# The slots layer of a decoder kernel issued in small parts between the half steps of the first cross attention

## The chip, the cores and the metric

The kernel runs on one core of one Trainium2 chip. The metric is the device time of one execution in microseconds (us). Five engines of the core work side by side, each through its own queue of instructions: PE (TensorE, matrix products and transposes), DVE (VectorE), ACT (ScalarE), POOL (GpSimd) and SP (SyncE, which here only starts transfers).

## The reference, cut to what matters

The input x has 64 batches of 128 rows and 256 columns, and all is fp32 but for two quantized products at the end. Six layers follow each other, each in the form x = x + layer(layernorm(x)):

```
x = x + window_attention(ln(x))          # stage A
x = x + cross_attention_0(ln(x), ctx)    # stage B: 16 heads of 16, mask, output projection
x = x + slots(ln(x))                     # stage C
x = x + causal_attention(ln(x))          # stage D: bias from a small net over positions
x = x + cross_attention_1(ln(x), ctx)    # stage E
x = x + bit_linear_ffn(ln(x))            # stage F
```

The slots layer (C) routes each row to 64 slots and writes back from them. For each batch:

```
h      = gelu(x @ w1' + c1)                       # 128 wide
logits = (h @ w2' + b2) / (|tau| + 0.1)           # 64 slots
alpha  = softmax over the top 8 logits, 0 elsewhere
gi     = (alpha^T @ x) / column sums of alpha     # 64 x 256
r, z   = sigmoid(...), n = tanh(...)              # a GRU step from gi and the fixed slot state
out    = alpha @ ((new slot state) @ wv' ) @ wo' + bo
```

No value of one batch enters another batch in any of the layers, so the slots layer of a batch needs only the cross attention of the same batch.

## The kernel before

**Groups and stages.** The 64 batches are held in SBUF as 16 tiles `x[g]` of four batches (`GB` = 4). The stages run one after the other, each over all groups, and each changes `x[g]` in place. Each has its own pools of SBUF and PSUM buffers. The program is written against a layer that records instructions, finds their dependences, sets the semaphores and gives out buffers; it also decides the order of the instructions on each engine, by priority (the order of the program's text) and by what its own plan holds to be ready. So an instruction may stand earlier on its engine than the text has it, but on the chip each engine works through that fixed order.

**Stage B, cross attention 0.** `stage_cross0` calls `attention_stage`, a software pipeline in half steps `j` = 0 to 136. A half step handles half of the heads (two of four row blocks) of a batch. In half step `j`:

- `score_burst` (L409) issues 32 small products into one PSUM tile `sc` of four banks: for batch `j // 2` the scores whose row maxima are needed, and for the batch three half steps older the transposed scores with the maxima already subtracted. Pool `scB` has one such tile, so a burst waits until the tile has been read.
- `score_max` (DVE, L424 `negmax`) reads two banks of it, `score_exp` (ACT, L438 `e`) the other two.
- Then come, for older batches, `weigh_values` (L459, at odd `j`), `divide` (L471 to L478), `turn_output` (L488) and `finish_batch` (L140, then the add into x at L619), each with a PSUM tile of the pool `ps`, which has four.
- At even `j`, `start` calls `prep` of the next batch: normalize the query (L594), copies on POOL (L599 to L604), eight transposes (L612) and two copies on ACT (L615). For the first batch of a group it also computes the group's layer norm statistics (`ln_stats`, L97 to L100, with a power on POOL), from which DVE takes `r4` (L588).
- At odd `j`, `shift_query` (L447, L451) waits for the maxima and makes the shifted query `q2`.

A batch is finished in half step 2n + 8. One group of four batches is eight half steps.

**Stage C, slots.** `stage_slots` runs over groups: `slots_route(g)`, then the two `slots_update` generators of group g - 1 (one for each pair of batches), which are advanced in turn. `slots_route` normalizes (L107), adds `bo` to x on POOL (L723), transposes (`transpose_group`, L119), projects and applies Gelu (L131, L731), makes the logits (L734 to L743), picks the top eight (L748, L749) and forms the softmax (L750 to L759, with an Exp at L754). `slots_update` has six parts between its `yield`s: u1 the sums into slots (L770), u2 their division (L776 to L779), u3 transposes, the copy `giT` and the products with `wih` (L783 to L798), u4 the gates on DVE, POOL and ACT (L802 to L810), u5 transposes, the copy `sT` and the product with `wvo` (L814 to L822), u6 the product with alpha and the add into x (L826, L831). Gelu and Exp belong to different activation tables, so ACT loads a table before each (L731 and L754).

**Stage D's start.** `prep_fire` builds a bias table: position differences on POOL (`Iota`, L895 and L899), absolute value, logarithm and relu on ACT (L904 to L911), a product on DVE (L910), 128 small products on PE (L918) and the adds on DVE (L926). Its tiles lie in SBUF that the stages before it used.

**Constants.** `prep_window`, `prep_cross0`, `prep_proj(.., "e")`, `prep_bitnet` and `prep_slots` load and prepare weights ahead of stage A. SP starts the transfers.

Of the kernel before, what the change touches and what calls it, by code (L numbers as in the profile page):

```python
# [16 lines left out]
D = 256  # L17
H = 16
DH = 16
S = 128  # L20
# [61 lines left out]
def psum(k):  # L82
    return k.ps.tile([128, 512], F, tag="ps", name="ps")
# [412 lines left out]
    b.fin(py[:, 0:D])  # L496


def attention_stage(k, pool, w1, prep, wo, lay, bias_s=None, bias_t=None):

    nms = []
    for i in range(2):
        t = w1.tile([S, lay.size], F, name=f"negmax{i}")
        k.nc.gpsimd.memset(t, 0.0)
        nms.append(t)
    bs = {}  # L510

    def start(n):
        b = bs[n] = prep(n)
        b.lay = lay
        b.nm = nms[n % 2]
        b.e = [None, None]

    def at(j, lag):
        n, odd = divmod(j - lag, 2)
        return bs.get(n) if not odd else None  # L520

    start(0)
    for j in range(2 * k.NB + 9):
# [12 lines left out]
        if at(j, 6):  # L536
            divide(k, pool, at(j, 6))
        if at(j, 7):
            turn_output(k, pool, at(j, 7))
        if at(j, 8):  # L540
            finish_batch(k, bs.pop((j - 8) // 2), wo)
        if hf == 0 and n + 1 < k.NB:
            start(n + 1)
        if hf == 1 and n < k.NB:
            shift_query(k, pool, bs[n])

# [9 lines left out]
    return cx  # L556


def stage_cross0(k, w):
    nc = k.nc  # L560
    with k.tc.tile_pool(name="wb", bufs=2) as wp, k.tc.tile_pool(name="wb1", bufs=1) as w1, \
            k.tc.tile_pool(name="wb3", bufs=3) as w3:
        qps, kps, vas = [], [], []
        for i in range(2):
            qp = w1.tile([S, H, 32], F, name=f"qp{i}")
            nc.gpsimd.memset(qp, 0.0)
            nc.gpsimd.memset(qp[:, :, 17:18], 1.0)
            qps.append(qp)
            kp = w1.tile([S, H, 32], F, name=f"kp{i}")
            nc.gpsimd.memset(kp, 0.0)  # L570
            nc.gpsimd.memset(kp[:, :, 16:17], 1.0)
            kps.append(kp)
        for i in range(4):
            va = w1.tile([S, H, 32], F, name=f"va{i}")
            nc.gpsimd.memset(va, 0.0)
            nc.gpsimd.memset(va[:, :, 16:17], 1.0)
            vas.append(va)
        cxs = {0: load_group(k, wp, 0)}
        stats = {}

        def prep(bi):
            g, b = divmod(bi, GB)
            if b == 0:
                if g + 1 < k.G:
                    cxs[g + 1] = load_group(k, wp, g + 1)
                mv, rs = ln_stats(k, wp, g)
                r4 = wp.tile([S, GB], F, tag="r4", name="r4")
                nc.vector.tensor_scalar(r4, rs, 0.25, None, ALU.mult)  # L588
# [12 lines left out]
            cv = cxs[g][:, b, :].rearrange("p (h d) -> p h d", d=DH)  # L601
            nc.gpsimd.tensor_copy(kp[:, :, 0:DH], cv)
            nc.gpsimd.tensor_copy(kp[:, :, 17], w.mbias[:, bi : bi + 1].to_broadcast([S, H]))
            nc.gpsimd.tensor_scalar(va[:, :, 0:DH], cv, mk, None, ALU.mult)  # L604
            t = Batch()
            t.qt = w3.tile([128, 4, S], F, tag="qt", name="qt")
            t.kt = w3.tile([128, 4, S], F, tag="kt", name="kt")
            for src, dst in ((qp, t.qt), (kp, t.kt)):
                p = psum(k)
                sf = src.rearrange("p h i -> p (h i)")  # L610
                for c in range(4):
                    nc.tensor.transpose(  # L612
                        p[:, c * S : (c + 1) * S], sf[:, c * 128 : (c + 1) * 128], k.ident
                    )
                nc.scalar.copy(dst, p.rearrange("p (c l) -> p c l", l=S))  # L615
            t.va, t.row_scale = va, mk

            def fin(y):
                nc.vector.scalar_tensor_tensor(xb, y, mk, xb, ALU.mult, ALU.add)  # L619

            t.fin = fin
            return t

        attention_stage(k, wp, w1, prep, w.wp, Heads(False))


def prep_cross0(k, pool):
# [87 lines left out]
    return w  # L715


def slots_route(k, w, g, wp):
    nc = k.nc
    xn = wp.tile([S, GB, D + 1], F, tag="xn", name="xn")  # L720
# [5 lines left out]
    xnT = wp.tile([128, 2, GB * S], F, tag="xnT", name="xnT")  # L726
    transpose_group(k, xn, xnT)
    p = psum(k)
    project(k, p, w.w1, 0, 128, xnT, 0, GB * S)
    hT = wp.tile([128, GB * S], F, tag="hT", name="hT")  # L730
    nc.scalar.activation(hT, p, AF.Gelu, bias=w.c1[:, 0:1])  # L731
    p = psum(k)
# [5 lines left out]
    lg = wp.tile([S, GB, SLOTS], F, tag="lg", name="lg")  # L738
# [4 lines left out]
    nc.vector.tensor_scalar(lg, lg, w.itau[:, 0:1], None, ALU.mult)  # L743
    m8 = wp.tile([S, GB, 8], F, tag="m8", name="m8")
    al = wp.tile([S, GB, SLOTS], F, tag="al", name="al")
    e = wp.tile([S, GB, SLOTS], F, tag="e", name="e")
    for b in range(GB):
        nc.vector.max(m8[:, b], lg[:, b])  # L748
        nc.vector.match_replace(al[:, b], m8[:, b], lg[:, b], -3.0e38)  # L749
    nc.vector.tensor_tensor(al, al, lg, ALU.not_equal)  # L750
    nc.vector.tensor_tensor(
        e, lg, m8[:, :, 0:1].to_broadcast([S, GB, SLOTS]), ALU.subtract
    )
    nc.scalar.activation(e, e, AF.Exp)  # L754
    nc.vector.tensor_tensor(al, al, e, ALU.mult)
    den = wp.tile([S, GB], F, tag="den", name="den")
    nc.vector.tensor_reduce(den, al, AX.X, ALU.add)
# [7 lines left out]
def slots_update(k, w, g, xn, al, pb, wp):  # L765
# [67 lines left out]

def stage_slots(k, w):
    with k.tc.tile_pool(name="wc", bufs=2) as wp, k.tc.tile_pool(name="wc4", bufs=4) as wq:
        prev = None
        for g in range(k.G + 1):
            cur = slots_route(k, w, g, wp) if g < k.G else None
            if prev is not None:
                parts = [slots_update(k, w, g - 1, *prev, pb, wq) for pb in range(GB // 2)]  # L840
                while parts:
                    parts = [q for q in parts if next(q, q) is not q]
            prev = cur

# [410 lines left out]
def decoder(tc, a, stages="ABCDEF"):  # L1255
# [152 lines left out]
```

## Time and profile before

| what | us |
|---|---|
| median of 3 runs (3829.28 to 3832.84) | 3831.49 |
| the profiled execution, its own time | 3831.31 |
| its span, first to last instruction | 3829.5 |
| stage B, from the first memsets of its buffers to the last add into x | 612 to 1183 |
| stage C, to the last add into x | 1183 to 1634 |
| preparation of stage D, to its first statistics | 1634 to 1697 |

A row of the timeline reads: start, duration, engine, line, operation, output <- input, and in brackets the idle time of the engine ahead of it with what ended it. A row of the waits reads: who waited for whom, us in total, how many times, the longest. A row of the windows reads: the stretch, its length, busy us of PE, PE's weight load, DVE, ACT and POOL with the number of instructions, the granted TensorE clock as a share of full speed, DMA share and GB/s. Durations of neighbours overlap by some 0.1 us, so two starts are the better measure of what an instruction takes of its engine.

### The profile page before, as it was taken

Reading aid. Unit: us, or ns where it says so; the run is one execution under the profiler, and the core shown is the slowest. Engines: PE = TensorE matmul, PEld = TensorE weight load, DVE = VectorE, ACT = ScalarE, POOL = GpSimd, SP = SyncE. Lnnn points to the kernel's source line nnn. Section 1 sums busy time; section 2 is a strip of 40 time slices with the busy share of each in tenths; the row PEclk is TensorE's granted clock in tenths of the full one; section 3 lists DMA queues with packets and bytes.
Section 4 is the critical chain, followed back from the end, with each engine's and each line's share of the span. In section 5 each row is a group of like instructions: output and inputs, shape, how many; then the busy total and the mean of one; then the engine's idle time right before and its main releaser. Section 6 shows DMA issues by size and latency. Waiting matters only on the chain.

```text
span 3829.5 us, 65173 instructions
## 1 busy us (share of the span) xinstructions
PE 2986.5 (78%) x27764; PEld 1889.1 (49%) x27764; DVE 2602.7 (68%) x4843; ACT 1279.2 (33%) x1882; POOL 1063.4 (28%) x1048
## 2 busy tenths in 40 slices
PE   4888885888887766658888888888888985776676
PEld 1333333666664333345666666666666762333333
DVE  5888766666666555447888777765556557887766
ACT  1111111444443232323333333334444543332332
POOL 3555553343332222130000000020001004534434
PEclk9898986999998888968999999899999997888887
DMA  5000000000000000000000000000000000000000
GB/s 182 1 1 1 1 1 17 18 18 13 18 13 1 1 1 1 1 15 1 1 2 1 1 2 1 2 28 13 13 13 18 13 2 6 11 11 17 11 17 17
DMA packets 40817, 48.09 MB, mean 13 GB/s; under 512 B 4448, under 2 KB 37616, under 8 KB 40272
## 3 DMA queue, kind: packets, MB, share of 16 engines
q1 hardware_dynamic: 39872, 42.17, 3.4%
q8 instruction: 220, 3.60, 0.4%
q0 software_dynamic: 656, 1.75, 0.2%
q14 instruction: 69, 0.57, 0.0%
HBM read 35.52 MB, written 8.39 MB: 11 GB/s over the span
## 4 chain that ended last, share of the span: by engine, by line
PE 29%; DVE 20%; ACT 3%; POOL 3%; issue 1%; DMA 0%; DVEq 0%; POOLq 0%; ACTq 0%; SPq 0%
PE sc L409 7%; PE ps L131 6%; PE cv L1142 4%; DVE uq L1194 3%; PE ps L140 3%; DVE negmax L424 3%; PE ps L990 3%; DVE sb L422 3%; DVE e L436 2%; POOL dg L1088 2%; PE ps L447 2%; PE ps L471 1%; PE ps L459 1%; DVE xn L107 1%; ACT e L438 1%
## 5 line engine op out<-in xcount | busy, mean ns | idle before, releaser
L409 PE MATMUL sc<-kt,qt 32*128 32x128 f32 x6144 | 508.6, 297 | 164.1 <-DVE e L436 104.7
L409 PEld LDWEIGHTS sc<-kt,qt 32*128 32x128 f32 x6144 | 421.0, 197 | 306.5 <-issue 177.3
L424 DVE TENSOR_REDUCE negmax<-sc 128x8 f32<-128x1024 f32 x256 | 313.3, 1224 | 298.7 <-PE sc L409 298.7
L409 PE MATMUL sc<-q,kt 32*128 32x128 f32 x6144 | 510.4, 298 | 1.9 <-DVE e L436 1.6
L409 PEld LDWEIGHTS sc<-q,kt 32*128 32x128 f32 x6144 | 421.0, 197 | 4.7 <-issue 2.9
L438 ACT ACTIVATE e<-sc 128x1024 f32<-128x1024 f32 x256 | 263.2, 1028 | 223.1 <-DVE negmax L424 214.5
L1142 PE MATMUL cv<-hp,taps 128*128 128x512 f32 x480 | 258.0, 687 | 86.9 <-DVE hp L1132 81.3
L260 POOL TENSOR_TENSOR pr<-pad,qt 128x896 f32<-128x896 f32 x128 | 243.8, 1940 | 211.4 <-ACT pad L247 211.4
L451 DVE TENSOR_TENSOR q<-ps,qt 128x512 f32<-128x512 f32 x192 | 132.7, 691 | 154.2 <-PE ps L447 151.9
L438 ACT ACTIVATE e<-e 128x1024 f32<-128x1024 f32 x128 | 135.3, 1057 | 284.7 <-DVE e L436 284.7
L447 PE MATMUL ps<-ident,negmax 128*128 128x128 f32 x768 | 131.7, 297 | 125.8 <-DVE negmax L424 123.9
L464 ACT COPY avs<-ps 128x512 f32<-128x512 f32 x192 | 112.5, 586 | 338.7 <-PE ps L459 338.7
L422 DVE TENSOR_TENSOR sb<-sc,bias_s 128x1024 f32<-128x1024 f32 x128 | 156.6, 1223 | 97.0 <-PE sc L409 97.0
L1142 PEld LDWEIGHTS cv<-hp,taps 128*128 128x128 f32 x480 | 103.0, 222 | 216.1 <-issue 111.0
L958 POOL TENSOR_TENSOR x<-x,t_d_bo 128x1024 f32<-128x1024 f32 x16 | 37.6, 2350 | 561.9 <-DVE xn L107 561.9
L318 DVE TENSOR_TENSOR pv<-sc,pad 128x896 f32<-128x896 f32 x128 | 137.1, 1083 | 75.9 <-PE sc L312 75.9
L1193 POOL TENSOR_TENSOR hs<-hs,s2b 128x512 f32<-128x512 f32 x128 | 171.2, 1372 | 9.8 <-ACT s2b L1185 9.8
L958 POOL TENSOR_TENSOR x<-x,t_e_bo 128x1024 f32<-128x1024 f32 x16 | 37.5, 2346 | 489.8 <-DVE xn L107 489.8
L447 PEld LDWEIGHTS ps<-ident,negmax 128*128 128x128 f32 x768 | 85.4, 147 | 168.0 <-DVE negmax L424 95.3
L1194 DVE TENSOR_SCALAR uq<-hs 128x512 bf16<-128x512 f32 x128 | 152.9, 1228 | 10.2 <-POOL hs L1193 10.2
L436 DVE TENSOR_TENSOR e<-sc,bias_t 128x1024 f32<-128x1024 f32 x128 | 155.6, 1216 | 5.2 <-PE sc L409 5.1
L424 DVE TENSOR_REDUCE negmax<-sb 128x8 f32<-128x1024 f32 x128 | 155.0, 1211 | 0.1
(323 smaller groups left out, 6593.2 us busy)
## 6 DMA issues: line engine op xcount, KB each, us to landing
cx<-in_ctx_dram SPq DMA_DIRECT2D x32, 512.0 KB, 3.8
x<-in_x_dram SPq DMA_DIRECT2D x16, 512.0 KB, 9.2
out_dram<-x SPq DMA_DIRECT2D x16, 512.0 KB, 2.9
t_g_w<-in_g_w_dram SPq DMA_DIRECT2D x2, 1024.0 KB, 6.9
t_c_wih<-in_c_wih_dram SPq DMA_DIRECT2D x1, 768.0 KB, 5.4
t_c_whh<-in_c_whh_dram SPq DMA_DIRECT2D x1, 768.0 KB, 7.8
t_a_cw<-in_a_cw_dram SPq DMA_DIRECT2D x1, 448.0 KB, 10.6
t_c_bih<-in_c_bih_dram POOLq DMA_DIRECT2D x1, 384.0 KB, 4.4
```

Of the source, the lines that this page charges most:

```text
L131: k.nc.tensor.matmul(out, w[:, kc, c0 : c0 + cn], rhsT[:, kc, n0 : n0 + n], start=(kc == 0), stop=(kc == 1),)
L260: k.nc.gpsimd.tensor_tensor(pr[:, c], shift_windows(t.kt, b, c), t.qt[:, c, b, :].unsqueeze(1).to_broadcast([128, WIN, S]), ALU.mult,)
L318: nc.vector.tensor_tensor(pv, bc[th][:, :, 0 : WIN * 64].rearrange("p c (l w) -> p c l w", w=WIN), shift_windows2(t.vt, b, th), ALU.mult,)
L409: k.nc.tensor.matmul(t[:, side * 2 + rr, c * S : (c + 1) * S], st[rows, c, :], mv[rows, c, :], start=True, stop=True,)
L422: nc.vector.tensor_tensor(sb, src, bias_s[:, hf * 2 : hf * 2 + 2, :], ALU.add)
L424: nc.vector.tensor_reduce(b.lay.extra(b.nm, hf * 2), src.rearrange("p r (c m) -> p r c m", m=S), AX.X, ALU.max, negate=True,)
L436: nc.vector.tensor_tensor(e, src, bias_t[:, hf * 2 : hf * 2 + 2, :], ALU.add)
L438: nc.scalar.activation(e, src, AF.Exp)
L447: nc.tensor.transpose(pt[:, c * S : (c + 1) * S], b.nm[:, b.lay.base[c] : b.lay.base[c] + S], k.ident)
L1142: nc.tensor.matmul(pc, w.taps[:, CONV_PE.index(j), t, :], hp[:, :, t : t + S], start=(t == 0), stop=(t == 2),)
L1193: nc.gpsimd.tensor_tensor(hs[:, j], hs[:, j], s2b, ALU.mult)
L1194: nc.vector.tensor_scalar(uq[:, j], hs[:, j], MAGIC, MAGIC, ALU.add, ALU.subtract)
```

## The change

`slots_route` becomes a generator of seven parts (r1 to r7), and a class `Slots` advances it and the two update generators by one part each in a `tick`, which `attention_stage` calls at the end of each half step. The route of group g starts in half step 8g + 15, one after its last batch has been finished, and its updates seven half steps later, so each half step carries at most one route part and one update part of two neighbouring groups. In terms of `j` modulo 8 the ticks hold: 7: u2, r1; 0: u3, r2; 1: u4, r3; 2: u5, r4; 3: u6, r5; 4: r6; 5: r7; 6: u1. What is left when the half steps are over is run by `finish`.

The last product of an update goes into two tiles of `ps` and is added to x in two instructions; before it took one `sc` tile of two banks and one add for both batches. Some slots tiles have one buffer where they had two, and the update's have two where they had four. The stage C loop goes. The constants of stage A get a pool of their own, which ends with that stage, and `prep_proj(.., "e")` is called after the cross attention.

```
-def attention_stage(k, pool, w1, prep, wo, lay, bias_s=None, bias_t=None):
+def attention_stage(k, pool, w1, prep, wo, lay, bias_s=None, bias_t=None, tick=None):
...
         if hf == 1 and n < k.NB:
             shift_query(k, pool, bs[n])
+        if tick is not None:
+            tick(j)
...
-        attention_stage(k, wp, w1, prep, w.wp, Heads(False))
+        slots = Slots(k, wc, c2, w1)
+        attention_stage(k, wp, w1, prep, w.wp, Heads(False), tick=slots.tick)
+        slots.finish()
...
-def slots_route(k, w, g, wp):
+def slots_route(k, w, g, wp, w1):
...
+    yield        # six of them: after bo, the transposes, Gelu, the logits, the top 8, Exp
...
-    po = psum2(k)
     for j in range(2):
+        po = psum(k)
         nc.tensor.matmul(
-            po[:, j, 0:D], giT[64 * j : 64 * j + 64, 2, :], sv[64 * j : 64 * j + 64, :],
+            po[:, 0:D], giT[64 * j : 64 * j + 64, 2, :], sv[64 * j : 64 * j + 64, :],
             start=True, stop=True,
         )
-    xs = k.x[g][:, pb * 2 : pb * 2 + 2, :]
-    nc.vector.tensor_tensor(xs, po[:, :, 0:D], xs, ALU.add)
...
+        xb = k.x[g][:, pb * 2 + j, :]
+        nc.vector.tensor_tensor(xb, po[:, 0:D], xb, ALU.add)
+
+
+class Slots:
...
+    def __init__(self, k, w, pool, w1):
+        self.k, self.w, self.pool, self.w1 = k, w, pool, w1
+        self.g = 0
+        self.routing, self.updating, self.routed = None, [], None
+
+    def tick(self, j):
+        k = self.k
+        if self.routing is None and self.g < k.G and j > 2 * (GB * self.g + GB - 1) + 8:
+            self.routing = slots_route(k, self.w, self.g, self.pool, self.w1)
+        self.updating = [q for q in self.updating if next(q, q) is not q]
+        if self.routing is not None:
+            try:
+                next(self.routing)
+            except StopIteration as stop:
+                self.updating = [
+                    slots_update(k, self.w, self.g, *stop.value, pb, self.pool)
+                    for pb in range(GB // 2)
+                ]
+                self.routing = None
+                self.g += 1
+
+    def finish(self):
+        while self.g < self.k.G or self.updating:
+            self.tick(1 << 30)
...
         with tc.tile_pool(name="w0", bufs=1) as w0:
-            with scores("psP", 4) as k.ps:
-                wa = prep_window(k, w0)
-                wb = prep_cross0(k, w0)
-                we = prep_proj(k, k.res, "e")
-                wf = prep_bitnet(k, k.res)
-                wc = prep_slots(k, w0)
-            with scores("psA", 3) as k.ps, scores("s1A", 1) as k.s1, scores("scA", 2) as k.sc:
-                stage_window(k, wa)
+            with tc.tile_pool(name="wA", bufs=1) as wA:
+                with scores("psP", 4) as k.ps:
+                    wa = prep_window(k, wA)
+                    wb = prep_cross0(k, w0)
+                    wf = prep_bitnet(k, k.res)
+                    wc = prep_slots(k, w0)
+                with scores("psA", 3) as k.ps, scores("s1A", 1) as k.s1, scores("scA", 2) as k.sc:
+                    stage_window(k, wa)
             k.ps = ctx.enter_context(scores("ps", 4))
-            if "B" in stages:
-                with scores("scB", 1) as k.sc:
-                    stage_cross0(k, wb)
-            if "C" in stages:
-                with scores("scC", 2) as k.sc:
-                    stage_slots(k, wc)
+            with scores("scB", 1) as k.sc:
+                stage_cross0(k, wb, wc)
+        we = prep_proj(k, k.res, "e")
```

More of the change, by code (lines that the diff above doesn't have):

```diff
@@ L556, in load_group, with stage_cross0 @@
     return cx
-def stage_cross0(k, w):
+def stage_cross0(k, w, wc):
     nc = k.nc
     with k.tc.tile_pool(name="wb", bufs=2) as wp, k.tc.tile_pool(name="wb1", bufs=1) as w1, \
-            k.tc.tile_pool(name="wb3", bufs=3) as w3:
+            k.tc.tile_pool(name="wb3", bufs=3) as w3, k.tc.tile_pool(name="wc2", bufs=2) as c2:
         qps, kps, vas = [], [], []
@@ L715, in prep_slots @@
     return w
-def slots_route(k, w, g, wp):
+def slots_route(k, w, g, wp, w1):
     nc = k.nc
-    xn = wp.tile([S, GB, D + 1], F, tag="xn", name="xn")
+    xn = wp.tile([S, GB, D + 1], F, tag="c_xn", name="c_xn")
     nc.gpsimd.memset(xn[:, :, D : D + 1], 1.0)
@@ L725, in slots_route @@
     )
-    xnT = wp.tile([128, 2, GB * S], F, tag="xnT", name="xnT")
+    yield
+    xnT = w1.tile([128, 2, GB * S], F, tag="c_xnT", name="c_xnT")
     transpose_group(k, xn, xnT)
+    yield
     p = psum(k)
     project(k, p, w.w1, 0, 128, xnT, 0, GB * S)
-    hT = wp.tile([128, GB * S], F, tag="hT", name="hT")
+    hT = w1.tile([128, GB * S], F, tag="hT", name="hT")
     nc.scalar.activation(hT, p, AF.Gelu, bias=w.c1[:, 0:1])
+    yield
     p = psum(k)
@@ L737, in slots_route @@
         )
-    lg = wp.tile([S, GB, SLOTS], F, tag="lg", name="lg")
+    lg = w1.tile([S, GB, SLOTS], F, tag="c_lg", name="c_lg")
     nc.vector.tensor_tensor(
@@ L743, in slots_route @@
     nc.vector.tensor_scalar(lg, lg, w.itau[:, 0:1], None, ALU.mult)
+    yield
     m8 = wp.tile([S, GB, 8], F, tag="m8", name="m8")
-    al = wp.tile([S, GB, SLOTS], F, tag="al", name="al")
-    e = wp.tile([S, GB, SLOTS], F, tag="e", name="e")
+    al = wp.tile([S, GB, SLOTS], F, tag="c_al", name="c_al")
+    e = w1.tile([S, GB, SLOTS], F, tag="c_e", name="c_e")
     for b in range(GB):
@@ L749, in slots_route @@
         nc.vector.match_replace(al[:, b], m8[:, b], lg[:, b], -3.0e38)
+    yield
     nc.vector.tensor_tensor(al, al, lg, ALU.not_equal)
@@ L754, in slots_route @@
     nc.scalar.activation(e, e, AF.Exp)
+    yield
     nc.vector.tensor_tensor(al, al, e, ALU.mult)
@@ L823, in slots_update @@
     yield
-    po = psum2(k)
     for j in range(2):
+        po = psum(k)
         nc.tensor.matmul(
-            po[:, j, 0:D], giT[64 * j : 64 * j + 64, 2, :], sv[64 * j : 64 * j + 64, :],
+            po[:, 0:D], giT[64 * j : 64 * j + 64, 2, :], sv[64 * j : 64 * j + 64, :],
             start=True, stop=True,
         )
-    xs = k.x[g][:, pb * 2 : pb * 2 + 2, :]
-    nc.vector.tensor_tensor(xs, po[:, :, 0:D], xs, ALU.add)
[L834 to L843, printed above, removed]
+        xb = k.x[g][:, pb * 2 + j, :]
[23 more added lines that the diff above has]
+            self.tick(1 << 30)
 def prep_proj(k, pool, s):
```

## The prediction

> **What bounds the kernel now.** I read the windows first, for what each stage leaves free.
>
> ```profile
> 660.00:1130.00 470.00, 398.55 (x6560) 311.09 (x6560) 290.89 (x565) 211.77 (x334) 190.66 (x291) 0.98 0.05 16
> 1216.00:1590.00 374.00, 255.25 (x932) 139.50 (x931) 213.81 (x659) 115.67 (x200) 84.42 (x93) 0.87 0.00 1
> ```
>
> The first stretch is stage B, the second stage C. POOL's power L100 comes once a group: from 670.16 to 875.32 us in B six times (34.2 us a group), from 1242.12 to 1528.34 in C ten times (28.6). So a group costs 62.8 us, and by these rows its busy time is PE 29.0 + 19.5, DVE 21.2 + 16.3, ACT 15.4 + 8.8, POOL 13.9 + 6.5. No engine is full; the waits tell why.
>
> ```profile
> DVE negmax L424 <- PE sc L409: 102.4, 97, 2.5
> PEld sc L409 <- ACT e L438: 53.7, 98, 1.6
> DVE r L588 <- POOL ln_rs L100: 22.8, 13, 2.0
> ACT e L438 <- DVE negmax L424: 21.7, 13, 1.8
> ```
>
> B is a ring: burst (PE, 1.16 us), maxima (DVE, 1.2), exponential (ACT, 1.0), next burst, as there is one `sc` tile. ACT's timeline shows the beat:
>
> ```profile
> 903.87 1.03 ACT L438 ACTIVATE e<-sc 128x1024 f32<-128x1024 f32 x1
> ...
> 907.91 1.03 ACT L438 ACTIVATE e<-sc 128x1024 f32<-128x1024 f32 x1
> ...
> 913.62 1.02 ACT L438 ACTIVATE e<-sc 128x1024 f32<-128x1024 f32 x1 [1.82 <-DVE negmax L424]
> ```
>
> The usual half step takes 3.8 to 4.0 us; once a group it takes 5.7, where the maxima stand on DVE behind `r`, which waits for POOL's power. PE does the other products in the 2.6 us between bursts.
>
> C is bound by its chain of engines: in its waits the largest of ACT, DVE and PE are `rz` 75.9 us, `lg` 56.6 and 41.8 for `giT`. The last group shows the chain of u3 and u4 undisturbed:
>
> ```profile
> 1619.68 0.69 DVE L797 TENSOR_TENSOR rz<-ps,c_crz 128x512 f32<-128x512 f32 x1 [2.70 <-PE ps L140]
> ...
> 1623.71 0.43 DVE L807 SCALAR_TENSOR_TENSOR rg<-rz,rg 128x256 f32<-128x256 f32 x1 [2.15 <-POOL rg L806]
> 1624.24 0.43 DVE L810 SCALAR_TENSOR_TENSOR nn<-rg,nn 128x256 f32<-128x256 f32 x1
> 1624.58 0.68 DVE L797 TENSOR_TENSOR rz<-ps,c_crz 128x512 f32<-128x512 f32 x1
> ...
> 1629.13 0.43 DVE L810 SCALAR_TENSOR_TENSOR nn<-rg,nn 128x256 f32<-128x256 f32 x1
> ```
>
> The second generator's `rz` stands on DVE behind the first one's `nn`, so from the first `wih` product (1617.66) to the second `nn` it takes 11.9 us.
>
> **What the Trainium skill says.** "PSUM — Partial Sum Buffer", Engine vs sequencer instructions: the queues of DVE, ACT and POOL are strict FIFO, and matmuls start and complete in program order. The rows above agree (`negmax` behind `r`, 1.7 us). So a slots part placed ahead of `negmax` or `e` stops the ring. "ScalarE: Activation LUTs", What ACT_TABLE_LOAD costs: some 1283 ns, and with a drain 2.66 us. The trace has 1283 ns twice a group in C, and Gelu starts 1.3 us after its load begins (1594.23, 1595.52), so I take 1.28. Table sets, same page: exp and tanh share a set. So it was in C, where no load stands ahead of Tanh after Exp; B's exponentials then need a reload after each Gelu only. "TensorE: Matmul & The Clock Gate", What's actually happening: the clock follows recent activity. B's 0.98 against C's 0.87 fits; a mixed stage should lie between.
>
> **The change, part by part.** I walk one group of the mixed steady state with traced durations, through the order in which the changed program's instructions stand on each engine. Zero is the start of `e` in half step 0 (`j` modulo 8).
>
> Half step 0 to 1 (u3, r2). ACT does `e`, `qt`, `kt`, `giT` (end 2.4). PE has issued six of the 16 pieces of the next burst and then stands at the `wih` products, which wait for `giT`. Then come the 11.9 us of the chain above: the second half of the burst stands behind the second `wih` products and r2's eight transposes (1.04 us; in the cover of the chain), and `negmax` stands on DVE behind the second `nn`: 14.3. Maxima and latency 1.4: the next `e` at **15.7**, where before this step took 5.7 (its wait for `r` is now hidden, as `rz` is ready no sooner).
>
> Half step 1 to 2 (u4 counted above, r3): PE makes the query shift, then r3's product (1.8 us) ahead of the burst; ACT loads Gelu's table, runs it (0.69) and reloads (1.28), some 3.3 us beside burst and maxima (2.5): **4.9**.
>
> 2 to 3 (u5, r4): PE cuts the burst again at two products that wait for `sT` (ACT, behind `e`, `qt`, `kt`): two times 0.9 us of products plus some 0.8 of waiting, then the logits (1.0); on DVE `sv`, `lg` and half of the top eight stand ahead of `negmax` (1.5): **9.2**.
>
> 3 to 4 (u6, r5): on DVE four adds into x (0.42 each, where two of 0.69 were) and the softmax (about 1.5) stand ahead of `negmax`: **5.5**. Exp (0.42) lies on an ACT that waits.
>
> 4 to 5, 5 to 6 (r6, r7: no more left to do), 7 to 0: **3.8, 3.7, 3.7**. 6 to 7 (u1 1.0 on PE; r1's POOL power and four normalizations 1.4 on DVE ahead of `negmax`): **5.1**.
>
> The sum is 51.6 us, 17.4 over B's 34.2. C's whole PE work without pipeline fill is 14.8 us a group (wih 2 x 2.7, transposes 2.4, r3 1.8, logits 1.0, u1 1.0, wvo 1.8, u6 1.4), so PE alone asks 28.5 (its 398.55 us over the 112 exponentials of the stretch, times 8) + 14.8 = 43.3: the floor of a period. Latencies I did not see could add 5; a clock of 0.87 instead of 0.98 would add 9% of PE's share, some 4. I take 47 to 57.
>
> The end. The last maxima of B (1166.56 before) come with `j` = 127. From there, u2 to u6 of group 13 and all of group 14's route share the queue with B's own drain (16.2 us before): a C period of 28.6 plus 5, some 34 us, to the statistics of group 15 (bounds 27 to 45). From these to stage D's first statistics: the order now has D's four `Iota` pairs and the logarithms between the last groups' updates, since D's tiles no longer all wait for C's weights. POOL needs 4 x 3.85 + 2.35 + 3 x 0.75 = 20; ACT 3.7 + 3.6 + about 2 for table and `sT`; DVE 4.4 (L910); ACT 3.8; then PE 26.7 for the small products with group 15's updates (11) between, and 5 for the last adds and starts: 77 (60 to 90). Before, this preparation alone took 64, all after C.
>
> The start. Constants E move off it (1 MB), but SP now issues three more x tiles (1.5 MB) ahead of the `g_w` loads, on which DVE waited 5.94 us; at the 218 GB/s of the first 80 us this is some 2.3 us later; I take 3 (-5 to 8). SP's later transfers and POOL's row loads for E lie 1000 us ahead of their use in E: nothing.
>
> Sum, to D's first statistics: 1166.6 + 3 + 5 (group 0's route, alone) + 13 periods x 17.4 = 226 + 34 + 77 = 1511.6, against 1697.1: **185.5 us less**. Stages D, E and F keep their code and order, so the profiled execution goes from 3831.3 to 3645.8. The median of the runs is 0.2 above that execution: 3646.
>
> **The rivals.** *The FIFO stalls mostly hide* (PE becomes the bound): if the chains of u3 and u5 find other PE work, a period nears 43.3, 13 x 8.3 = 108 less: 3538. For it: PE is the busiest of B. Against: the burst is cut and its pieces stand behind the waiting products. 12%.
>
> *The end does not overlap*: D's tiles still wait for C's weights, so the slots tail (30) and the preparation (64) are in series: 112 - 77 = 35 more: 3681; or the clock stays at 0.87 (13 x 4 = 52): 3698. 11%, most of it in the range.
>
> *Slower*: the ring is stopped more often than it is filled. The place is DVE between half steps 0 and 4, where `negmax` stands behind the gates, the top eight and the adds; each of these waits for ACT or POOL, and those stand behind attention's copies (`kp`, `xm`, `va`: 2.5 us a batch on POOL). The price in C itself: a `giT` that came late cost PE 2.91 us at 1323.44, and `al` held DVE 2.51 us. It decides from a period of 51.6 + 185.5 / 13 = 65.9, that is 14.3 us more than I walked: every cross-engine step of u2 to u6 late by some 1.5 us. At 68 it gives 3859. Against: half of a period's half steps carry next to nothing. 6%.
>
> *The change doesn't do what it says*: the scheduler could have moved the parts together; the order on the engines shows them spread as the text has them, so I give it no share of its own.
>
> **How the numbers follow.** My forecast, period 47 to 57 and the end's bounds, has 70%, near 3646: 3571 (13 x 4.6 = 60 and 15 for the end less) to 3736 (13 x 5.4 = 70 and 20 more). With the late end and the cold clock, faster is 0.93 with the 12% of the first rival; slower 0.06; within 0.2% (7.7 us, about what a measurement of this kernel tells from no change) 0.01. The range 3570 to 3735 leaves out the first rival and the slower one: 0.18 to 0.2.
>
> **What would show it.** Right: no stretch of stage C; POOL's power for groups in the mixed stage 51 us apart per group (two a group now); `e` intervals of about 15, 5, 9, 5 us and then four of about 4; `negmax` waiting on nothing of PE in half step 1 but standing behind `nn`; 32 table loads as before; `Iota` ahead of the last `nn`; stages D to F of unchanged length. Wrong: bursts whole and 6 us apart (first rival), or periods over 60 with `nn` and `giT` rows as the longest waits (slower).

## The result, and the profile after

The changed kernel takes **3773.18 us** (median of 4 runs, 3766.91 to 3775.23) against 3831.69 of the kernel before beside it: a ratio of 0.9848, 95% interval 0.9835 to 0.986. The forecast was 3646, with a range from 3570 to 3735: the sign was right, and a third of the gain came.

The profiled execution shows where. Stage D's first statistics come at 1636.64 us instead of 1697.08, 60.4 us sooner, and stages D to F keep their length within 3 us. The first exponential of stage B comes at 645.58 instead of 648.56. Then the period of a group, from the starts of `e` in half steps 22 to 126, is **59.0 us** instead of 33.5; the forecast had 51.6. With stage C's 28.6 us a group as the page of before had them, the two layers in series took 62, so a mixed period saves only 3 us.

A window of the changed kernel, in the mixed stage, answers to those of stages B and C (length, busy us of PE, PE's weight load, DVE, ACT, POOL, granted clock):

```profile
740.00:1440.00 700.00, 570.04 (x6350) 417.02 (x6354) 418.20 (x1118) 277.27 (x459) 232.22 (x327) 0.90 0.03 10
```

The mixed stage has a clock of 0.90, where stage B had 0.98. These are its waits (who waited for whom, us in all, times, longest):

```profile
ACT e L438 <- DVE negmax L424: 171.5, 69, 5.0
PE ps L447 <- DVE negmax L424: 81.6, 34, 3.4
...
DVE negmax L424 <- PE sc L409: 62.3, 43, 4.3
...
PEld sc L409 <- ACT e L438: 35.6, 57, 1.4
```

Before, the maxima waited for PE's burst and the burst for the exponential: a ring that PE set. Now the exponential waits for the maxima far longer than the maxima for PE: they stand behind slots instructions on DVE. And PE waits for the same maxima, at the query shift L447.

The windows of one period show the half steps. Each stretch runs from one `e` to the next, the first into half step 0 (`j` modulo 8), the last into 7:

```profile
1155.19:1160.28 5.09, 4.98 (x48) 4.30 (x49) 2.94 (x6) 1.29 (x3) 2.17 (x2) 0.66 0.00 0
1160.28:1176.15 15.87, 11.07 (x103) 7.34 (x101) 9.59 (x26) 5.78 (x11) 7.22 (x10) 1.00 0.01 2
1176.15:1184.03 7.88, 7.64 (x58) 5.13 (x58) 3.25 (x7) 4.54 (x6) 0.27 (x1) 0.78 0.00 0
1184.03:1194.65 10.62, 8.00 (x84) 6.07 (x84) 4.41 (x18) 3.22 (x6) 2.77 (x5) 0.84 0.01 2
1194.65:1200.48 5.83, 5.77 (x60) 4.31 (x60) 5.63 (x17) 1.60 (x3) 0.00 (x0) 1.00 0.28 90
1200.48:1204.27 3.79, 3.12 (x68) 2.32 (x69) 2.78 (x8) 2.47 (x4) 2.60 (x5) 1.00 0.01 4
1204.27:1207.92 3.65, 3.47 (x49) 2.96 (x49) 2.84 (x6) 1.30 (x4) 0.50 (x1) 1.00 0.00 0
1207.92:1214.43 6.51, 4.04 (x79) 2.78 (x77) 4.27 (x14) 3.31 (x7) 4.30 (x7) 0.95 0.01 3
```

PE looks 97 to 98% busy in the first and third of these, but at a clock of 0.66 and 0.78: it is slow, not full. The same steps of other periods show what the clock costs; below are the step into 0 once more and the step into 3 twice:

```profile
1099.17:1103.07 3.90, 3.79 (x51) 3.37 (x52) 2.98 (x6) 1.29 (x3) 2.18 (x2) 1.00 0.01 4
887.39:896.54 9.15, 6.49 (x84) 5.06 (x84) 4.41 (x18) 3.22 (x6) 2.78 (x5) 1.00 0.01 2
1419.68:1431.89 12.21, 9.58 (x84) 7.34 (x84) 4.42 (x18) 3.23 (x7) 2.78 (x5) 0.72 0.01 1
```

With the clock at 1.00 these steps take 3.90 and 9.15 us; the forecast had 3.7 and 9.2. In the ten periods from 880 to 1455 us each of the two had a clock of 1.00 in three; in the other seven the step into 0 took 4.8 to 5.5 us and the step into 3 10.6 to 12.7. The timeline of the step from 1 to 2 shows what comes ahead of a low clock (start, duration, then the idle time ahead in brackets):

```profile
1174.55 0.43 DVE L822 SCALAR_TENSOR_TENSOR nn<-rg,nn 128x256 f32<-128x256 f32 x1
1174.90 1.21 DVE L424 TENSOR_REDUCE negmax<-sc 128x8 f32<-128x1024 f32 x1
1176.15 1.02 ACT L438 ACTIVATE e<-sc 128x1024 f32<-128x1024 f32 x1 [2.49 <-DVE negmax L424]
1176.27 1.09 PE L447 MATMUL ps<-ident,negmax 128*128 128x128 f32 x4 [3.38 <-DVE negmax L424]
...
1177.14 3.11 PE L131 MATMUL ps<-c_xnT,c_w1x 128*128 128x512 f32 x4
...
1182.73 1.28 ACT L438 ACT_TABLE_LOAD   x1 [1.75 <-DVE negmax L424]
1184.03 1.02 ACT L438 ACTIVATE e<-sc 128x1024 f32<-128x1024 f32 x1
```

`negmax` follows the second `nn` at once, as forecast. PE has then idled 3.38 us at L447, and its next products run at a cold clock, that is, a lowered one: 1.09 us for the shift (0.66 at 1194.67, in a step with the clock at 1.00) and 3.11 for Gelu's product (forecast 1.8). Ahead of the two other cold steps PE waited less:

```profile
1155.30 0.71 PE L447 MATMUL ps<-ident,negmax 128*128 128x128 f32 x4 [2.57 <-DVE negmax L424]
...
1185.10 0.37 PE L409 MATMUL sc<-kt,qt 32*128 32x128 f32 x1 [1.19 <-ACT e L438]
```

The first wait stands at the start of the step into 0, the second in the step into 3, where the burst waits for an exponential that the reload made late. And the reload of Exp's table does not run while ACT idles: it stands behind the exponential's own wait, and its 1.28 us come on top.

### The profile page after: what moved, and what is told of

Read it like the earlier page. It is cut to its first block, busy times and chain, and to the rows that moved or that the text cites. A ratio compares the mean times of both kernels' runs of the same rounds, so it can differ in the third digit from the quotient of the medians.

```text
span 3772.2 us, 65003 instructions
## 1 busy us (share of the span) xinstructions
PE 2993.5 (79%) x27764; PEld 1928.4 (51%) x27764; DVE 2562.4 (68%) x4875; ACT 1274.6 (34%) x1883; POOL 1058.7 (28%) x1048
## 4 chain that ended last, share of the span: by engine, by line
PE 47%; DVE 32%; POOL 10%; ACT 7%; issue 3%; DMA 1%; SPq 0%; DVEq 0%; POOLq 0%; ACTq 0%
PE sc L409 10%; PE ps L131 9%; PE ps L140 7%; DVE negmax L424 6%; PE cv L1172 4%; DVE uq L1224 4%; PE ps L1020 3%; DVE sb L422 3%; PE ps L447 3%; ACT e L438 3%; DVE e L436 2%; POOL pr L260 2%; DVE pv L318 2%; PE ps L459 2%; DVE oT L322 2%
## 5 line engine op out<-in xcount | busy, mean ns | idle before, releaser
L409 PE MATMUL sc<-kt,qt 32*128 32x128 f32 x6144 | 549.0, 305 | 161.1 <-DVE e L436 104.7
L409 PEld LDWEIGHTS sc<-kt,qt 32*128 32x128 f32 x6144 | 446.9, 202 | 318.9 <-issue 196.1
L409 PE MATMUL sc<-q,kt 32*128 32x128 f32 x6144 | 545.0, 305 | 2.0 <-DVE e L436 1.6
L409 PEld LDWEIGHTS sc<-q,kt 32*128 32x128 f32 x6144 | 443.1, 202 | 13.2 <-issue 10.0
L447 PE MATMUL ps<-ident,negmax 128*128 128x128 f32 x768 | 135.9, 304 | 178.8 <-DVE negmax L424 176.9
L447 PEld LDWEIGHTS ps<-ident,negmax 128*128 128x128 f32 x768 | 88.6, 151 | 218.0 <-issue 140.0
## 6 DMA issues: line engine op xcount, KB each, us to landing
t_a_cw<-in_a_cw_dram SPq DMA_DIRECT2D x1, 448.0 KB, 10.6
```

The source lines that it names most:

```text
L409: k.nc.tensor.matmul(t[:, side * 2 + rr, c * S : (c + 1) * S], st[rows, c, :], mv[rows, c, :], start=True, stop=True,)
L447: nc.tensor.transpose(pt[:, c * S : (c + 1) * S], b.nm[:, b.lay.base[c] : b.lay.base[c] + S], k.ident)
```

## The experiments

Line numbers of the experiments' kernels differ by a few from those of the changed kernel; the names of the tiles are the same. A ratio is always to the kernel before, run beside it. The means of the steps from `e` to `e` over half steps 22 to 126 were, in us, each column a kernel:

| into | before | forecast | changed | E3 Tanh | E5 part first | E7 norm on POOL |
|---|---|---|---|---|---|---|
| 0 | 4.04 | 3.7 | 4.82 | 4.28 | 4.60 | 3.65 |
| 1 | 5.26 | 15.7 | 15.94 | 16.01 | 15.97 | 19.29 |
| 2 | 4.80 | 4.9 | 7.89 | 6.63 | 5.20 | 7.49 |
| 3 | 3.78 | 9.2 | 10.65 | 9.55 | 9.26 | 10.38 |
| 4 | 4.04 | 5.5 | 5.88 | 5.68 | 6.11 | 5.89 |
| 5 | 3.78 | 3.8 | 3.79 | 3.96 | 4.91 | 3.79 |
| 6 | 4.05 | 3.7 | 3.65 | 3.64 | 3.64 | 3.65 |
| 7 | 3.78 | 5.1 | 6.40 | 6.39 | 6.40 | 4.20 |
| period | 33.5 | 51.6 | 59.0 | 56.2 | 56.1 | 58.3 |

**E1, stage D's preparation made to wait for the slots' end.**

```
         nd = cp.tile([128, 32, S], F, name="nd")
+        nc.gpsimd.tensor_copy(pn[:, 0:1], k.x[k.G - 1][:, GB - 1, 0:1])
+        nc.gpsimd.tensor_copy(nd[:, :, 0], k.x[k.G - 1][:, GB - 1, 0:32])
```

> The changed kernel, in which the first column of the tiles pn and nd of stage D's preparation is first written from the last rows of x[15], so that the Iotas and all that follows them wait for the last slots add. The interleaved period stays. Theory 1 (the interleave itself gains next to nothing, 59.0 us a period against 33.5 + 28.2 in series, and the gain of 58 us is the preparation of stage D, 64 us, lying beside the slots tail): the gain goes, +55 us, 3828 us (3815 to 3840), with the first statistics of stage D some 63 us behind the last slots add. Theory 2 (the interleave gives the gain, the overlap at the end is small): 3790 us or less.

3790.98 us, ratio 0.9896 (0.9877 to 0.9915). Theory 1 fell: only some 18 us of the gain (0.9896 less 0.9848) are the overlap at the end; 40 come without it. The reading of the two traces that led to theory 1 was a trap. In the changed kernel the last slots add comes at 1630 us, as it does before, and so the two layers seemed to have gained nothing. But there D's preparation lies between the last groups' updates and holds them up. In E1 it does not, and the last slots add is at 1588.3: B and C alone end 45 us sooner, 6.7 of them already at the first exponential, so that the interleave itself brings 39. From the statistics of group 15 the slots tail takes 47 us alone and the preparation 64.5; together 111 in series, 94.5 overlapped.

**E2, the layout of buffers and constants alone.**

```
 # the kernel before, with
+            with tc.tile_pool(name="wA", bufs=1) as wA:
...
+                    wa = prep_window(k, wA)
...
+        we = prep_proj(k, k.res, "e")      # behind stage C
```

> The kernel before, with only the moves of buffers and constants: stage A's constants in a pool of their own, and the constants of stage E prepared after stage C. No interleave; stages B and C follow each other as before. In this order the Iotas of stage D's preparation stand between the last gates of group 15 instead of behind them. Theory 1 (the layout is what lets stage D's preparation begin before the slots end): 3 us less at the start, as the changed kernel showed, and some 20 to 35 us less at the end, as POOL's 20 us of Iotas and part of ACT's logarithms come earlier: 3803 us (3785 to 3815). Theory 2 (the layout alone is worth only the start): 3825 to 3831 us.

3821.66 us, ratio 0.9973 (0.9964 to 0.9982): 10 us less, between the two forecasts. The `Iota`s do come earlier, among the gates of group 15 (ACT's `nd` starts at 1639.04 instead of 1652.81). Of these 13.8 us, 4.8 were there at the first exponential, so the `Iota`s' place brought 9.

**E3, no change of tables in the route.** `AF.Gelu` becomes `AF.Tanh`. This leaves out the layer's own function, so it is only a measurement.

> The changed kernel with Tanh in place of Gelu in the route, so that the route's values are others: Tanh is in Exp's table set, and the two table loads a group go. Theory A (the loads stand on the ring: Gelu's load and run, then the reload behind the wait of the exponential, and make half step 1 to 2 7.9 us instead of 4.9): that half step falls by 1.3 to 3.3 us, the period to 56.5, 14 periods and the tail: 3735 us (3720 to 3757). Theory B (the loads lie beside PE's query shift, product and burst, and the half step is long for the cold TensorE clock alone): 3765 to 3775 us, the half step at 7 us or more.

3739.09 us, ratio 0.9757 (0.9735 to 0.9779): 34 us less than the changed kernel, theory A in size. The step into 2 loses 1.26 us, one table load of 1.28. Into 3 and 0 it also gains, 1.1 and 0.5, where nothing was taken away: the granted clock there rises (into 3 from 0.83 to 1.00, into 0 from 0.72 to 0.86, means of ten periods). With the reload the 1.2 us are gone too for which PE waited for `e` in the step into 3; in E3 that step ran at a clock of 1.00 in all periods.

**E4, the parts cut finer and the second generator four half steps later.**

```
     nc.scalar.copy(giT, ...)
+    yield
     prz = psum(k)
...
     nc.scalar.activation(rz, rz, AF.Tanh, scale=0.5)
+    yield                                   # the n product and nn = n + bin follow here
...
     nc.gpsimd.tensor_tensor(nn, nn, rg, ALU.add)
+    yield
     nc.scalar.activation(nn, nn, AF.Tanh)
     nc.gpsimd.tensor_tensor(rg, w.hs, nn, ALU.subtract)
+    yield
...
     nc.scalar.copy(sT, ...)
+    yield
     p = psum(k)
```

> The changed kernel with the same work cut finer: yields in u3 behind the copy giT and behind the tanh of rz, in u4 behind POOL's nn and behind POOL's rg, in u5 behind the copy sT, so that no part holds a product or a DVE instruction that waits for another engine in the same part; and the second update generator starts four half steps after the first (the first two half steps after the route). giT gets a third buffer. Theory 1 (the period is long because in-order queues stop the ring at u3 to u5; PE's work asks 43 us): period 46 us (44 to 50), 13 us less for 14 periods: 3595 us (3550 to 3660). Theory 2 (a period of 59 is the sum of the engines' work and colder clock, whatever the order): 3717 us or more.

3741.24 us, ratio 0.9769 (0.9753 to 0.9785), period 56.6: by its numbers theory 2, whose reason, the engines' work in whatever order, E6 will refute. The step into 1 fell from 15.9 to 8.2, but four others took 7.1 to 8.4. Its longest wait of PE is in the first row (700 us); the second row is the same wait in E6, told below (600 us):

```profile
PE ps L447 <- DVE negmax L424: 122.7, 49, 3.5
```

```profile
PE ps L447 <- DVE negmax L424: 51.4, 39, 2.9
```

PE stood 9.9 us a period at the query shift, with slots products ready behind it, and ran at a clock of 0.89. That led to E5 and E6.

**E5, the slots part ahead of the query shift.**

```
+        if tick is not None:
+            tick(j)
         if hf == 1 and n < k.NB:
             shift_query(k, pool, bs[n])
-        if tick is not None:
-            tick(j)
```

> The changed kernel, with the slots part of a half step issued ahead of the query shift instead of behind it, so that in odd half steps PE has the part's products (Gelu's two of 2.84 us among them) ahead of the transposes L447 that wait for negmax. Theory A (half step 1 to 2 takes 7.9 us instead of the 4.9 forecast because negmax, L447, Gelu's products and the next burst stand in series on PE): that half step falls to 5.5 us (5 to 6.2), the period to 56.6, 14 periods: 3740 us (3725 to 3756). Theory B (the shift only comes later, and what is won ahead of it is lost behind it): 3765 to 3780 us, that half step above 7 us.

3729.53 us, ratio 0.9741 (0.9719 to 0.9762): theory A. The step into 2 took 5.20 us, in the range given. The groups of instructions show the clock in one product (busy us, mean ns of one): first the changed kernel, then E5.

```profile
L131 PE MATMUL ps<-c_xnT,c_w1x 128*128 128x512 f32 x40 | 31.2, 927 | 0.0
```

```profile
L131 PE MATMUL ps<-c_xnT,c_w1x 128*128 128x512 f32 x44 | 20.7, 593 | 0.0
```

The same product costs 927 ns behind the wait and 593 ahead of it. The 2.7 us that the step won are more than this: the product also no longer stands between `negmax` and the next burst. The step into 3 fell to 9.26, the forecast's 9.2, with no edit in it.

**E6, E4 and E5 together.**

> The finely cut and staggered kernel (3741 us), with the slots part of a half step issued ahead of the query shift. In it L447 stands idle on PE for negmax some 12 us a period (122.7 and 32.0 us in 700), and the parts of odd half steps hold about 5.8 us of products. Theory A (PE lost these by its own order): period 56.6 to 51 us, 14 periods: 3660 us (3640 to 3700). Theory B (DVE sets the pace: the scheduler has drawn the slots instructions of later half steps ahead of negmax, so negmax is as late as before): 3715 us or more, the period above 55.

3604.83 us, ratio 0.9411 (0.9386 to 0.9436), period **47.2**: theory A, and more than it said. The two edits bring 32 and 44 us alone, and 168 together. The cut takes the waits out of the parts; the place ahead of the shift puts the whole products into the time in which PE would wait for `negmax` (at L447 it now stands 4.0 us a period). The window of 740 to 1340 us shows PE's part:

```profile
740.00:1340.00 600.00, 531.95 (x6831) 394.45 (x6821) 443.60 (x1186) 300.31 (x491) 250.32 (x342) 0.97 0.04 11
```

PE is busy 532 of 600 us at a clock of 0.97. That is 41.8 us of each period, near the 43.3 us that the forecast had as PE's floor.

**E7, the route's normalizations on POOL** (in place of DVE's L107, in the changed kernel).

```
-    layernorm(k, wp, g, xn)
+    mv, rs = ln_stats(k, wp, g)
+    for b in range(GB):
+        nc.gpsimd.tensor_scalar(xn[:, b, 0:D], k.x[g][:, b, :], mv[:, b, 0:1], rs[:, b : b + 1],
+                                ALU.subtract, ALU.mult)
```

> The changed kernel with the four normalizations of the route on POOL instead of DVE, so that DVE does not wait for POOL's power ahead of negmax. Theory A (half step 6 to 7 takes 6.4 us because DVE stands some 2 us at the power and then makes 1.4 us of normalizations): that half step falls to 4.4 us (4 to 5), 14 periods of 2 us: 3746 us (3735 to 3758). Theory B (POOL's four normalizations come so late that the route's transposes stop PE in the next half step): 3765 us or more, half step 7 to 0 or 0 to 1 longer by as much.

3766.79 us, ratio 0.9832 (0.9813 to 0.9851): no difference to the changed kernel that the intervals can tell. Both theories saw something. The step into 7 fell from 6.40 to 4.20 and the one into 0 from 4.82 to 3.65; the one into 1 rose by 3.35. The timeline and the waits of E7 show the wait:

```profile
1154.89 4.83 POOL L730 TENSOR_SCALAR c_xn<-x,ln_mv,ln_rs 128x256 f32<-128x256 f32 x4
...
1166.30 0.17 DVE L592 TENSOR_SCALAR r<-ln_rs 128x4 f32<-128x4 f32 x1 [3.78 <-POOL ln_rs L100]
...
1169.13 5.49 PE L140 MATMUL ps<-t_c_wih,giT 128*128 128x512 f32 x8 [4.30 <-ACT giT L808]
```

```profile
PEld ps L140 <- ACT giT L808: 52.8, 21, 4.5
```

The four took 4.83 us on POOL. The add of `bo`, attention's copies and its power came behind them, the power only at 1165.23. DVE waited for it at `r`, ahead of `rz`; the second `giT` stands on ACT behind `rz` (1168.61), and PE waited 4.30 us for it. In the same 600 us the changed kernel's products waited 17.9 us for `giT`, these 52.8. A wait moved off DVE became one of PE.

**E9, E6 with the normalizations on POOL.**

> The finely cut and staggered kernel with both edits: the slots part ahead of the query shift, and the route's normalizations on POOL. Theory A: the two gains add, 27 us below the fine kernel with the part ahead of the shift, 3633 us (3605 to 3680), period 49. Theory B (DVE sets the pace by what else stands ahead of negmax: logits, top eight and softmax in one half step, statistics, gates and copies in another): no more than 15 us below it.

3621.84 us, ratio 0.9455 (0.9434 to 0.9477): slower than E6 by some 0.4%. The gains did not add; theory B's words hold (not 15 us below E6), though it foresaw no loss, and the time lies in theory A's range only because E6 was faster than forecast. The step into 7 gained 2.5 us and the one into 1 lost 2.6, as in E7; period 48.7.

**E10, E6 without the later start of the second generator.**

```
-FIRST, LAG = 2, 4
+FIRST, LAG = 0, 0
```

> The finely cut kernel with the part ahead of the query shift (3605 us, period 47.2), but with both update generators of a group starting together, right after the route, as in the changed kernel; the cuts stay. Theory A (the cuts and the place ahead of the shift are what frees the ring; the stagger only evens out the half steps): period 50 us (48 to 52), 14 periods: 3645 us (3615 to 3675). Theory B (the stagger is what matters, since two generators in one part stand in each other's way on DVE, as the second rz behind the first nn): period above 54, 3700 us or more.

**3600.32 us**, ratio 0.9409 (0.9387 to 0.9432), period 47.9: no slower than E6, and 15 us below theory A's range. The later start is worth nothing; this is the simplest of the fast versions, and it beats both kernels.

**E12, the route's logits behind the maxima of an even half step** (E6 with a second `yield` behind r1 and `FIRST` at 1).

> The finely cut, staggered kernel with the part ahead of the query shift (3605 us, period 47.2), with the route's parts behind the first one half step later and the updates starting one half step sooner behind it, so that the logits, the top eight and the softmax (4.3 us of DVE) follow the maxima of an even half step, where DVE has 0.7 us of its own, and not those of an odd one, where it has 2.6 us. Theory A (DVE's work ahead of negmax sets the two long half steps): half step 2 to 3 falls from 7.1 to 5 us, 3 to 4 rises from 3.8 to 5: period 46 us, 3590 us (3575 to 3604). Theory B (PE, busy 41.8 of 47.2 us a period, sets it): 3600 to 3620 us.

3660.21 us, ratio 0.9573 (0.9545 to 0.9601), period 51.2: a miss for both. The steps into 3 and 4 took 7.7 and 7.5. The logits left the step into 3, but Gelu's table load, its run and the reload moved into it. In the step into 4, which grew by 3.7 us over E6, logits, top eight and softmax now stand on DVE ahead of `negmax`, which in the period at 1064.41 starts 6.2 us after the `e`. The adds into x came late as well, and PE's output products waited for them:

```profile
PEld ps L140 <- DVE x L623: 31.0, 12, 3.1
```

This wait falls into the step into 5, which grew by only 0.8 us, so it is the smaller part of the loss.

**E13 and E14, which of the cuts counts.** Both are E10 with some of its `yield`s taken out. E13 keeps those behind `giT` and `sT`; the gates are one part again. E14 keeps those in the gates; transposes, copy and products of u3, and of u5, are one part again.

> The finely cut kernel without stagger, the part ahead of the query shift (3600 us, period 47.9), with only the two cuts on PE's side kept (behind the copies giT and sT, so that no product waits inside a part) and the gates in one piece again: the copy, POOL's sum, tanh, POOL's difference and the last two DVE instructions of both generators in one part. Theory A (the gates on DVE, ahead of negmax, are the larger loss: each generator waits some 2 us for POOL and ACT there): period 53 us or more, 3680 us (3660 to 3720). Theory B (PE's stand at giT and sT is the larger loss): period 49 us or less, 3625 us or less.

> The same kernel (3600 us, period 47.9), with only the cuts in the gates and between rz and the n product kept, and transposes, copy and products together again in u3 and in u5, so that PE stands at giT and at sT in the middle of a burst. Theory A (the gates are the larger loss): period 50 us or less, 3640 us or less. Theory B (PE's stand at giT and sT is the larger loss, some 1 us for each of four copies and the burst cut by it): period 53 us or more, 3680 us or more.

E13: 3620.46 us, ratio 0.945 (0.9432 to 0.9469), period 48.5. E14: 3706.57 us, ratio 0.967 (0.9655 to 0.9684), period 54.4. Theory B in both by the numbers. Beside E5, which has neither kind of cut (3729.53), PE's cuts alone bring some 109 us, those in the gates alone some 23, both 129. The timeline of E14, then that of E13, shows the products that use `giT`:

```profile
1067.26 0.51 ACT L803 COPY giT<-ps 128x384 f32<-128x384 f32 x1
1067.82 1.98 PE L140 MATMUL ps<-t_c_wih,giT 128*128 128x512 f32 x4 [0.64 <-ACT giT L803]
...
1074.65 1.22 DVE L424 TENSOR_REDUCE negmax<-sc 128x8 f32<-128x1024 f32 x1
```

```profile
1085.32 5.33 PE L140 MATMUL ps<-t_c_wih,giT 128*128 128x512 f32 x16
...
1085.93 1.21 DVE L424 TENSOR_REDUCE negmax<-sc 128x8 f32<-128x1024 f32 x1
```

In E14 the products, each behind a copy, stand among the pieces of a burst: the `e` before it started at 1065.40, and the burst's maxima start 9.2 us later. In E13 all sixteen products run in one go behind a whole burst, and the maxima and the exponential of that burst run beside them. The standing itself is small, as a wait of E14 shows (600 us):

```profile
PEld ps L140 <- ACT giT L803: 12.2, 22, 0.8
```

That is some 1.1 us a period, of the 6.5 that E14 lost against E10. The larger part is the cut burst: its pieces stand behind slots products, so its maxima come late.

## Why the prediction was wrong

The sum was 125 us off: 185.5 us less were forecast, 60.4 came. The step that failed is the price of PE's products in the walk of a period: it took them warm throughout, and it hid a table load and a wait for POOL that stood in the ring. By its own terms:

- **The period: 13 x 8.1 = 105 us.** The increment was 59.0 - 33.5 = 25.5 us and not 17.4. Of this, 7.4 are in the half steps and 0.7 in the base (34.2 taken, 33.5 measured).
- **The end: 17.5 us.** 94.5 us from the statistics of group 15 to D's first statistics, where 77 stood.
- **Group 0's route alone:** 5.5 more (half steps 3 to 22 took 90.4 us, before 79.9; forecast 5 more). **The start:** 6 less (3 sooner instead of 3 later; in the experiments with the same start the first exponential lay between 632 and 648 us, so this sign is not settled). **From the last maxima to the statistics of group 15:** 35 us for 34.

**The steps of the period.** Into 1 was right: 15.7 forecast, 15.94 measured, with `negmax` behind the second `nn` as the walk had it. Into 4, 5 and 6 were right within 0.4. Four were mis-sized:

- *Into 2, 4.9 forecast, 7.89 measured.* The order was right: shift, product, burst, maxima, exponential. Three sizes were not. The shift and the product were taken at warm durations, 0.6 and 1.8 us; behind an idle PE they took 1.09 and 3.11. And the reload was counted "beside burst and maxima"; it ran behind the exponential's wait and cost 1.28. Together 3.1 us. E3 (1.26 less) shows the reload; E5 (2.7 less, the reload still there) shows the product's place, and its 593 ns the warm price.
- *Into 3, 9.2 forecast, 10.65 measured.* The changed kernel itself takes 9.15 in the periods with the clock at 1.00; E3 and E5 have 9.55 and 9.26, at 1.00 and 0.98, where its mean is 0.83. What was missing was the clock.
- *Into 7, 5.1 forecast, 6.40 measured.* The four normalizations were counted, but not DVE's wait for POOL's power ahead of them, some 2 us. E7 takes both away and has 4.20.
- *Into 0, 3.7 forecast, 4.82 measured,* at a clock of 0.72, and 3.90 with the clock at 1.00. E7 has 3.65 there: without the wait of DVE for POOL's power in the step into 7, PE does not idle at L447, and the step keeps its speed.

Of the 7.4 us in the half steps the clock is thus some 4.2 (1.8 into 2, 1.5 into 3, 0.9 into 0), the reload 1.3, the wait for POOL's power 1.3. The forecast had the clock as a rival worth 4 us a period, for a mean of 0.87 (its 9% was low: 0.98 to 0.87 is 13%). The mean was 0.90 and the price nearly as stated, but it belonged into the walk, since it falls on steps that set the ring, behind waits of PE that the ring itself makes.

"TensorE: Matmul & The Clock Gate", What's actually happening, has the clock go cold after at least one idle window of about 3.4 us. The 3.38 us at 1176.27 with 927 ns behind it, against 593, agree. But here the clock also fell behind shorter waits: in the step into 0 in seven of the nine periods in which PE had waited 2.6 us at L447, and in the step into 3 in seven of ten with 1.2 us at L409. Why it stayed up in the others was not tried.

**The end.** The order of work was right, the sizes of three terms were not. From 1542.08 us the `Iota`s with the gates between took until 1566.46, 24.4 us for 20. The DVE product ended 9.4 us after the logarithm, not 4.4, since logits and top eight of group 15 stood ahead of it. And from the last small product to D's first statistics it took 10.8 us, not 5. The 128 small products with the updates between took 37.8 us, as forecast (26.7 and 11). The terms as listed add up to 80 and not to 77, which is most of the rest.

**The rivals.** PE as the bound did not come true in this kernel, but it was a sound limit: E6 and E10 come within 5 us a period of the floor of 43.3. The slower case did not come: 59.0 stayed below its 65.9, and what the steps between half steps 0 and 4 took too long was mostly PE's clock and the reload, not the late ACT and POOL that it named. The rival that the clock stays low, 13 x 4 = 52 us, came nearly as priced: 13 x 4.2 = 55. That the end does not overlap was wrong: it overlaps, for 16 us. Its 112 us are not the sum of the 30 and 64 beside them, which is 94; but in series E1 measured 111.

## What to carry to other kernels

Cut interleaved work where an engine hands over to another, so that no part holds an instruction that waits for the same part; and issue it ahead of the instruction that waits in the host's loop, not behind it: here either edit alone brought 1%, both together 4.5%, and most of the cuts' gain came from those that keep a burst of PE whole. When you walk a ring by durations, look for the waits of PE that the ring makes and price the step behind each of them cold as well (here the clock fell behind waits of 1.2 to 3.4 us, though not behind each of them), and look where a table load stands in the queue before you hide it. Two ends that fall on the same microsecond don't prove that a stage gained nothing: take the overlap away and look again.

## What the runs showed of the hardware beyond that

POOL's `Iota` holds up some of DVE's instructions. The two timelines show the four normalizations of group 15: in the changed kernel an `Iota` runs beside them, in E1 it does not.

```profile
1543.15 4.87 DVE L107 TENSOR_SCALAR c_xn<-x,ln_mv,ln_rs 128x256 f32<-128x256 f32 x4 [1.82 <-POOL ln_rs L100]
1543.21 3.69 POOL L929 IOTA nd<- 32x4096 f32 x1
...
1555.31 3.69 POOL L929 IOTA nd<- 32x4096 f32 x1
1555.56 0.42 DVE L815 SCALAR_TENSOR_TENSOR rg<-rz,c_ghn 128x256 f32<-128x256 f32 x1
```

```profile
1542.61 1.38 DVE L107 TENSOR_SCALAR c_xn<-x,ln_mv,ln_rs 128x256 f32<-128x256 f32 x4 [1.81 <-POOL ln_rs L100]
```

4.87 us against 1.38: the difference is nearly the 3.69 us of the `Iota`. The gate `rg`, with two inputs from SBUF, took its usual 0.42 us beside another `Iota`; beside POOL's add of `bo` to x, at 1549.31, it took 1.42. "SBUF — State Buffer", SBUF: two separate sides, has DVE and POOL share a port pair that one of them holds for a whole instruction; DVE needs it in its two-port modes, and for an instruction of two SBUF inputs only against a POOL instruction that reads SBUF. An `Iota` reads nothing, the add reads x: all three fit, if the normalization runs in such a mode, which no run here shows by itself. A gate can still be late beside an `Iota`, behind another instruction that is held: `nn` at 1560.90 took 3.50 us behind a `TENSOR_SCALAR` (L933) that took 3.65 beside the fourth `Iota`.
